# Spline layer: the part right of the middle added to x by VectorE in twelve units of sixteen

## The chip, the cores and the metric

The program runs on one core of one Trainium2 chip. The metric is the time of one execution of the whole program on the device, in microseconds, as the median of three runs. A core has a matrix engine (TensorE, "PE" in the profile; its weight loads are "PEld"), a vector engine (VectorE, "DVE"), an activation engine (ScalarE, "ACT"), GpSimd ("POOL") and SyncE ("SP"), which here issues DMAs. Each works through its own queue in order, and they wait for each other by semaphores.

## The reference

A network of four layers on x, 8 images of 64 channels of 128x128, all float32. Each layer is x = x + f(gn(x)) with a group norm in front. The layer that matters here is the second, a spline per channel:

```
x = x + _L0_conv_ref(_gn(x), ...)          # adder layer, 3x3, relu(b - sum|patch - w|)
x = x + _L1_conv_ref(_gn(x), ...)          # spline layer
x = x + _L2_conv_ref(_gn(x), ...)          # Haar, depthwise, 1x1, 3x3, gelu, inverse Haar
x = x + _L3_conv_ref(_gn(x), ...)          # nearest of 512 vectors

def _L1_conv_ref(x, coef, scale_base, scale_sp, bias):
    basis = _bspline_basis(xcl[..., None], grid)        # cubic, 8 functions on 12 knots
    spline = jnp.einsum('bhwck,ck->bhwc', basis, coef)
    out = scale_base * jax.nn.silu(xcl) + scale_sp * spline + bias
```

## The kernel before, in words

The eight images are worked on as four pairs: two images of 64 channels fill the 128 partitions. `run` takes a pair through layer 0, beside which the layers 2 and 3 of the pair before run as a list of steps, and then through layer 1 (`layer1`), which runs alone. After the last pair, layers 2 and 3 run by themselves. So layer 1 makes four separate stages in the profile. In layer 0 the order of the instructions on PE, ACT and DVE is written out by hand; in layer 1 it is left to the framework's scheduler, which orders each engine's queue by its own estimate, so that the instructions of `end` don't stand where the program has them.

Layer 1 cuts a pair's 128x128 pixels into 16 units of 8 rows (1024 pixels; 128x1024 per tile). The spline is even and odd about its middle: with z = |distance from the middle|, six truncated cubes of z serve the left and the right half. A tile holds one image, its 64 channels twice, so that the upper 64 partitions take knots 0 to 2 and the lower ones knots 3 to 5. For each unit and each of two images:

- z by ACT (L794) from xd, which DMA brings in (L747, four DMAs of 256 KB a unit, three buffers; beside them x itself, 1024 KB for two units);
- for three pairs of knots (p = 0, 1, 2) the truncated difference r, by ACT as a ReLU (L803) or by DVE as min and subtract (L805); its square by ACT into r3 (L806); and the cube r3 = r3 * r by DVE (L807). r has three buffers, r3 five;
- products by PE (L818): the cubes times coefficients into two PSUM tiles, `pa` (what holds left of the middle) and `pb` (what is added right of it), two buffers each. In float32 a product appears as two matmul records; those of the two images stand beside each other in halves of the array. With the second knot pair (p = 1) go the products of silu (L812, ACT) into `pa` (L820).

`end(n)` finishes a unit, and is called in the middle of the next one, after its second knot pair: DVE makes u = (x >= mean) * pb (L772), PE adds u to `pa` by a product with the identity (L774), and DVE writes x = pa + bias + x (L775). Two units make a chunk: after the second, DVE takes its statistics (L450, four instructions), and a chunk's x is stored by a DMA (L780). u has one buffer. In the last unit `end` stands by itself at the end of the stage.

Of the kernel before, what the change touches and what calls it, by code (L numbers as in the profile page):

```python
# [16 lines left out]
ALU = mybir.AluOpType  # L17
# [13 lines left out]
NQ = 6  # L31
# [69 lines left out]
class Net:  # L101
# [627 lines left out]
    def layer1(self, mr, stats, nxt):  # L729
        nc, tc = self.nc, self.tc  # L730
        N = R * W // 2
        images = [slice(i * C, (i + 1) * C) for i in range(2)]
        with ExitStack() as ctx:
            sp = ctx.enter_context(tc.tile_pool(name="l1", bufs=2))
            xdp = ctx.enter_context(tc.tile_pool(name="l1_xd", bufs=3))
            cp = ctx.enter_context(tc.tile_pool(name="l1_c", bufs=1))
            pp = ctx.enter_context(tc.tile_pool(name="l1_ps", bufs=2, space=PSUM))

            def unit(n):
                return self.x[n // 2][:, n % 2 * R // 2 : (n % 2 + 1) * R // 2, :].rearrange("p r w -> p (r w)")  # L740

            def twice(n):

                xd = xdp.tile([P, 2, N], F32, name="xd")
                for i in range(2):
                    for h in range(2):
                        nc.sync.dma_start(out=xd[images[h], i, :], in_=self.x_of[0][images[i], n * N : (n + 1) * N])  # L747
                if n % 2 == 0:
                    self.x.append(self.load(n // 2))
                return xd  # L750

            l1w = cp.tile([P, L1W], F32, name="l1w")
            nc.sync.dma_start(out=l1w, in_=self.l1w_dram)
            dspl = l1w[:, 0 : 10 * C].rearrange("p (k n c) -> p k n c", k=2, n=5)
            dbase, of_image = l1w[:, 10 * C : 12 * C], l1w[:, 12 * C :].rearrange("p (i n) -> p i n", i=2)
            self.x = []
            xds = [twice(n) for n in range(3)]

            sb = cp.tile([P, 2], F32, name="sb")
            nc.vector.tensor_copy(sb[:, 0:1], mr[:, 1:2])  # L760
            nc.vector.tensor_scalar(sb[:, 1:2], mr[:, 0:1], mr[:, 1:2], -1.0, ALU.mult, ALU.mult)
            zb = cp.tile([P, 2, 2], F32, name="zb")
            for i in range(2):
                pm = pp.tile([P, 2, 512], F32, name="pm", tag="pa")
                nc.tensor.matmul(pm[:, 0, 0:2], of_image[:, i, :], sb, start=True, stop=True)
                nc.vector.tensor_scalar(zb[:, i, :], pm[:, 0, 0:2], 2.5, None, ALU.mult)

            def end(n, pa, pb):

                xv = unit(n)  # L770
                u = sp.tile([P, N], F32, name="u", bufs=1)
                nc.vector.scalar_tensor_tensor(u, xv, mr[:, 0:1], pb.rearrange("p q n -> p (q n)"), ALU.is_ge, ALU.mult)  # L772
                for q in range(2):
                    nc.tensor.matmul(pa[:, q, :], self.ident, u[:, q * 512 : (q + 1) * 512], start=False, stop=True)  # L774
                nc.vector.scalar_tensor_tensor(xv, pa.rearrange("p q n -> p (q n)"), self.bias1, xv, ALU.add, ALU.add)  # L775
                if n % 2 == 1:
                    j = n // 2
                    self.chunk_stats(stats, j)
                    if nxt is not None:
                        nc.sync.dma_start(out=self.x_of[1][:, j * R * W : (j + 1) * R * W], in_=self.x[j].rearrange("p r w -> p (r w)"))  # L780

            late = None
            for n in range(2 * NCH):
                xv = unit(n)

                def work(name, bufs=2):
                    return sp.tile([P, N], F32, name=name, tag=name, bufs=bufs)

                pa = pp.tile([P, 2, 512], F32, name="pa")
                pb = pp.tile([P, 2, 512], F32, name="pb")  # L790
                zs = []
                for i in range(2):
                    z = work(f"z{i}")
                    nc.scalar.activation(z, xds[n][:, i, :], AF.Abs, bias=zb[:, i, 1:2], scale=zb[:, i, 0:1])  # L794
                    zs.append(z)
                for p in range(NQ // 2):
                    cubes, ws = [], []
                    for i in range(2):
                        r, r3 = work("r", 3), work("r3", 5)
                        kn = self.knots[:, p : p + 1]  # L800
                        on_act = p < 1 + i
                        if on_act:
                            nc.scalar.activation(r, zs[i], AF.Relu, bias=kn, scale=-1.0)  # L803
                        else:
                            nc.vector.tensor_scalar(r, zs[i], kn, kn, ALU.min, ALU.subtract)  # L805
                        nc.scalar.activation(r3, r, AF.Square)  # L806
                        nc.vector.tensor_tensor(r3, r3, r, ALU.mult)  # L807
                        cubes.append(r3)
                        ws.append(p + 3 if on_act else p)
                    if p == 0:  # L810
                        sl = work("sl")
                        nc.scalar.activation(sl, xv, AF.Silu, bias=sb[:, 1:2], scale=sb[:, 0:1])  # L812
                    for q in range(2):
                        cols = slice(q * 512, (q + 1) * 512)
                        for k, to in enumerate((pa, pb)):
                            for i in range(2):
                                stop = k == 1 and p == NQ // 2 - 1
                                nc.tensor.matmul(to[images[i], q, :], dspl[:, k, ws[i], :], cubes[i][:, cols], start=(p == 0), stop=stop)  # L818
                        if p == 1:
                            nc.tensor.matmul(pa[:, q, :], dbase, sl[:, cols], start=False, stop=False)  # L820
                    if p == 1 and late is not None:
                        end(*late)
                late = (n, pa, pb)
                if n == 4 and nxt is not None:
                    self.pad_first(nxt)
                if n + 3 < 2 * NCH:
                    xds.append(twice(n + 3))
            end(*late)


# [536 lines left out]
```

## Time and profile before

| | |
|---|---|
| time of three runs | 19147.62, 19152.85, 19155.82 us; median 19152.85 |
| profiled execution | span 19147.4 us from first to last instruction; no other time is shown for it |
| PE busy | 18332.0 us (96%) |
| DVE busy | 17951.2 us (94%) |
| ACT busy | 17340.8 us (91%) |
| POOL busy | 2778.2 us (15%) |
| L774 (identity product) | 256 matmul records, 592 ns median |
| L772, L775 (DVE, 128x1024 with PSUM) | 64 each, 1272 and 1284 ns median |
| L807 (DVE, 128x1024, two inputs in SBUF) | 384, 1218 ns median |
| wait of L775 for L774 | 91.3 us in 60 waits |

The page adds up an engine's busy time over the whole span, which here is an average over layer-0 stretches, four layer-1 stages and a tail. A matmul's duration includes its way through the array, and the next one starts before it ends; DVE and ACT instructions overlap a little, too. So what an instruction takes from its engine is read from the distance between starts, and a stage is looked at by itself. "issue" is idle time in which nothing visible was waited for.

### The profile page before, as it was taken

The numbers are of one execution on the slowest core, as the hardware profiler recorded it, in microseconds if no ns is written. First come the engines' busy times: TensorE is split into PE (matmuls) and PEld (weight loads), VectorE is DVE, ScalarE is ACT, GpSimd is POOL, SyncE is SP. The second block draws the span as 40 slices with busy tenths as digits, with TensorE's granted clock in tenths as the row PEclk, the third lists the DMA queues.
The fourth block names the chain that finished last, engine by engine and source line by source line (L and its number), as shares of the span: only waits on it lengthen the run. The fifth ranks groups of instructions, "written<-read, shape, count | busy, mean of one in ns | idle before, by whom it ended". The sixth has DMA issues, their size and how long they took to land.

```text
span 19147.4 us, 330733 instructions
## 1 busy us (share of the span) xinstructions
PE 18332.0 (96%) x146698; PEld 5818.3 (30%) x146698; DVE 17951.2 (94%) x13918; ACT 17340.8 (91%) x6457; POOL 2778.2 (15%) x1663
## 2 busy tenths in 40 slices
PE   8999999999999999999999999999999999999977
PEld 2333233232233222222222322222232323222263
DVE  8999999989999999998999999999899999999867
ACT  7999999889999999988999999998899999999803
POOL 0000000000000244300000034420000003442005
PEclk9999999999999999999999999999999999999986
DMA  2000000121111001021111100002011110000231
GB/s 66 6 11 10 6 10 8 40 68 32 40 34 33 25 18 29 25 61 48 34 42 30 33 21 24 23 28 78 29 35 41 35 34 16 22 25 13 62 96 39
DMA packets 425513, 636.07 MB, mean 33 GB/s; under 512 B 65168, under 2 KB 314640, under 8 KB 399120
## 3 DMA queue, kind: packets, MB, share of 16 engines
q1 hardware_dynamic: 368272, 549.81, 9.5%
q0 software_dynamic: 55808, 65.11, 1.9%
q8 instruction: 1149, 18.83, 0.4%
q14 instruction: 284, 2.33, 0.0%
HBM read 485.16 MB, written 129.54 MB: 32 GB/s over the span
## 4 chain that ended last, share of the span: by engine, by line
PE 53%; DVE 28%; issue 10%; ACT 8%; DMA 1%; SPq 0%; POOL 0%; DVEq 0%; ACTq 0%; POOLq 0%
PE ps L722 39%; DVE buf L655 12%; DVE buf L659 9%; ACT buf L653 7%; PE cv L1139 5%; PE pa L818 2%; PE pb L818 2%; DVE dw L1116 1%; DVE nd L1264 1%; DVE ix L1266 1%; DVE dw L897 1%; PE py L1162 1%; DVE x L655 1%; ACT t L1254 1%; PE pd L1252 1%
## 5 line engine op out<-in xcount | busy, mean ns | idle before, releaser
L722 PE MATMUL ps<-buf,sel 128*32 128x512 f32 x116336 | 13030.5, 597 | 371.1 <-DVE buf L659 234.2
L653 ACT ACTIVATE buf<-buf,w 128x4096 f32<-128x4096 f32 x1980 | 7213.9, 3710 | 301.8 <-PE ps L722 295.3
L653 ACT ACTIVATE buf<-x,w 128x4096 f32<-128x4096 f32 x1938 | 7046.2, 3710 | 347.0 <-PE ps L722 288.0
L722 PEld LDWEIGHTS ps<-buf,sel 128*32 128x32 f32 x116336 | 3625.9, 110 | 9365.5 <-issue 7898.4
L655 DVE TENSOR_SCALAR buf<-buf,w 128x4096 f32<-128x4096 f32 x1795 | 4162.2, 2356 | 188.7 <-PE ps L722 187.5
L655 DVE TENSOR_SCALAR buf<-x,w 128x4096 f32<-128x4096 f32 x1558 | 3639.5, 2366 | 287.4 <-PE ps L722 271.2
L659 DVE SCALAR_TENSOR_TENSOR buf<-buf,w,buf 128x2048 f32<-128x2048 f32 x1262 | 2913.4, 2348 | 22.9
L659 DVE SCALAR_TENSOR_TENSOR buf<-x,w,buf 128x2048 f32<-128x2048 f32 x1072 | 2475.3, 2349 | 19.7
L1267 POOL DMA_INDIRECT g<-in_L_conv_embed_weight,ix x768 | 1832.8, 2386 | 2840.3 <-issue 1400.3
L633 POOL DMA_DIRECT2D y<-in_x x480 | 608.8, 2099 | 9431.2 <-ACT y L620 6457.2
L1139 PE MATMUL cv<-dw,w2s 64*128 64x512 f32 x6912 | 1654.0, 606 | 3.2 <-issue 3.2
L653 ACT ACTIVATE x<-buf,w 128x4096 f32<-128x4096 f32 x396 | 1468.9, 3709 | 59.3 <-PE ps L722 59.3
L722 PE MATMUL ps<-x,sel 128*32 128x512 f32 x10832 | 1303.0, 594 | 27.1 <-DVE x L659 18.5
L1139 PEld LDWEIGHTS cv<-dw,w2s 64*128 64x128 f32 x6912 | 627.4, 186 | 1025.4 <-issue 1011.1
L655 DVE TENSOR_SCALAR x<-buf,w 128x4096 f32<-128x4096 f32 x281 | 659.9, 2348 | 24.6 <-PE ps L722 24.4
L722 PEld LDWEIGHTS ps<-x,sel 128*32 128x32 f32 x10832 | 350.8, 110 | 851.1 <-issue 747.5
L1116 DVE SCALAR_TENSOR_TENSOR dw<-sub,dws,dw 128x512 f32<-128x512 f32 (+2 forms) x768 | 574.5, 748 | 10.6
L1264 DVE CUSTOM_DVE_ANT_0 nd<-pd,t 128x512 f32<-128x512 f32 x768 | 519.8, 677 | 31.0 <-ACT t L1254 31.0
L807 DVE TENSOR_TENSOR r<-r,r 128x1024 f32<-128x1024 f32 x384 | 454.9, 1218 | 80.2 <-ACT r L806 72.2
L1266 DVE FIND_INDEX8 ix<-best,nd 128x8 uint32<-128x512 f32 x768 | 526.1, 685 | 0.1
L1252 PE MATMUL pd<-embT,xn 64*128 64x512 f32 x1536 | 490.1, 650 | 29.1 <-DVE best L1264 28.7
L1254 ACT ACTIVATE t<-esq_half,xsq 128x512 f32<-128x512 f32 x768 | 510.8, 717 | 3.1 <-DVE best L1264 3.1
(239 smaller groups left out, 7891.7 us busy)
## 6 DMA issues: line engine op xcount, KB each, us to landing
w2s<-w_dram SPq DMA_DIRECT2D x576, 192.0 KB
xd<-x_dram SPq DMA_DIRECT2D x256, 256.0 KB
x<-x_dram SPq DMA_DIRECT2D x56, 1024.0 KB
u<-u_dram SPq DMA_DIRECT2D x64, 768.0 KB
raw<-in_x SPq DMA_DIRECT2D x32, 1024.0 KB
x_dram<-y SPq DMA_DIRECT2D x512, 64.0 KB
out<-x SPq DMA_DIRECT2D x32, 1024.0 KB
y<-in_x POOLq DMA_DIRECT2D x480, 64.0 KB, 4.2
```

The costliest lines, as they stand in the source:

```text
L653: nc.scalar.activation(ab, tap(j, ts[0]), AF.Abs, bias=w[:, ts[0] : ts[0] + 1], scale=-1.0)
L655: nc.vector.tensor_scalar(ab, tap(j, ts[0]), w[:, ts[0] : ts[0] + 1], None, ALU.max)
L659: nc.vector.scalar_tensor_tensor(at, tap(j, t, h), w[:, t : t + 1], at, ALU.max, ALU.add)
L722: nc.tensor.matmul(at, sel[:, M - 1 - m : 3 * M - 1 - m], rhs, start=(n == first[p]), stop=(n + 1 == first[p + 1]))
L818: nc.tensor.matmul(to[images[i], q, :], dspl[:, k, ws[i], :], cubes[i][:, cols], start=(p == 0), stop=stop)
L1116: nc.vector.scalar_tensor_tensor(out, v, wt, out, ALU.mult, ALU.add)
L1139: nc.tensor.matmul(ps[:, i], weights[r, w // 3, :], v, start=(k == 0 and n == 0), stop=(k == 3 and n == 8))
L1252: nc.tensor.matmul(ps, xns[j][at, r, :], self.embT[at, :], start=True, stop=True)
L1254: nc.scalar.activation(t, self.esq_half, AF.Identity, bias=xsqs[j][:, n : n + 1])
L1264: nc.vector.tensor_tensor_reduce(nd, ps, t, 1.0, -FAR, ALU.subtract, ALU.max, mx[:, 0:1])
L1266: nc.vector.max_index(ix, mx, nd)
L1267: nc.gpsimd.indirect_dma_start(out=g[:, img, :], out_offset=None, in_=self.embed, in_offset=bass.IndirectOffsetOnAxis(ap=ix[:, 0:1], axis=0),)
```

## The change

In twelve of sixteen units (all but 3, 7, 11 and 15) DVE adds x to u in place, and L775 adds that sum instead of x; the product with the identity is left out. In those units the last product of the third knot pair into `pa` is marked as the one that ends the sum. Nothing else is edited.

```diff
+            def on_array(n):
+                return n % 4 == 3
+
             def end(n, pa, pb):
 
                 xv = unit(n)
                 u = sp.tile([P, N], F32, name="u", bufs=1)
                 nc.vector.scalar_tensor_tensor(u, xv, mr[:, 0:1], pb.rearrange("p q n -> p (q n)"), ALU.is_ge, ALU.mult)
-                for q in range(2):
-                    nc.tensor.matmul(pa[:, q, :], self.ident, u[:, q * 512 : (q + 1) * 512], start=False, stop=True)
-                nc.vector.scalar_tensor_tensor(xv, pa.rearrange("p q n -> p (q n)"), self.bias1, xv, ALU.add, ALU.add)
+                if on_array(n):
+                    for q in range(2):
+                        nc.tensor.matmul(pa[:, q, :], self.ident, u[:, q * 512 : (q + 1) * 512], start=False, stop=True)
+                    plus = xv
+                else:
+                    nc.vector.tensor_tensor(u, u, xv, ALU.add)
+                    plus = u
+                nc.vector.scalar_tensor_tensor(xv, pa.rearrange("p q n -> p (q n)"), self.bias1, plus, ALU.add, ALU.add)
...
-                                stop = k == 1 and p == NQ // 2 - 1
+                                stop = p == NQ // 2 - 1 and (k == 1 or not on_array(n))
```

## The prediction

> **What bounds the kernel now.** I first read the page's chain by line: the layer-1 matmuls of L818 have 4% of the 19147.4 us span, the adder layer's (L722) 39%. So the change can touch only the four stages of the spline layer. The table by stretches, asked for those four, says how large they are and who is busy:
>
> ```profile
> core 0: us, PE busy (x) PEld busy (x) DVE busy (x) ACT busy (x) POOL busy (x), PEclk, DMA share, GB/s
> 3801.00:4049.00 248.00, 240.40 (x896) 78.19 (x896) 203.34 (x206) 200.77 (x193) 0.00 (x0) 0.98 0.47 135
> 17922.00:18168.00 246.00, 236.81 (x896) 77.49 (x896) 203.48 (x207) 197.81 (x191) 0.91 (x5) 0.98 0.36 94
> ```
>
> About 990 us in all; TensorE (PE) is busy nearly throughout, VectorE (DVE) and ScalarE (ACT) some 82%. Busy matmuls are pipelined, so the chain of waits has to confirm it. Inside a stage it runs on PE alone; one unit of it:
>
> ```profile
> 3999.99 0.86 PE pb L818 x4
> 4000.85 0.86 PE pa L818 x4
> ...
> 4009.28 1.06 PE pa L820 x2
> 4010.34 1.72 PE pa L774 x4
> 4012.05 1.01 PE pa L818 x4
> ```
>
> The identity product (L774) is four matmul records, 1.72 us, on the path. DVE's timeline of the same unit shows what it does meanwhile and what it waits for (in brackets):
>
> ```profile
> 4001.96 1.27 DVE L772 SCALAR_TENSOR_TENSOR u<-x,mr,pb 128x1024 f32<-128x1024 f32 x1
> 4003.15 1.22 DVE L807 TENSOR_TENSOR r<-r,r 128x1024 f32<-128x1024 f32 x1
> 4004.29 1.53 DVE L805 TENSOR_SCALAR r<-z,knots 128x1024 f32<-128x1024 f32 x2
> 4006.54 3.50 DVE L807 TENSOR_TENSOR r<-r,r 128x1024 f32<-128x1024 f32 x3 [0.72 <-ACT r L806]
> 4009.95 0.81 DVE L805 TENSOR_SCALAR r<-z,knots 128x1024 f32<-128x1024 f32 x1
> 4012.09 1.28 DVE L775 SCALAR_TENSOR_TENSOR x<-pa,bias,x 128x1024 f32<-128x1024 f32 x1 [1.33 <-PE pa L774]
> 4013.29 2.35 DVE L807 TENSOR_TENSOR r<-r,r 128x1024 f32<-128x1024 f32 x2
> 4015.56 0.69 DVE L450 BATCH_NORM_STATS2 stats<-x 128x6 f32<-128x512 f32 x1
> 4016.16 1.27 DVE L772 SCALAR_TENSOR_TENSOR u<-x,mr,pb 128x1024 f32<-128x1024 f32 x1
> ```
>
> L775 starts at 3982.88, 3997.31, 4012.09, 4026.52: a unit takes 14.43 or 14.78 us, 14.61 in the mean. The extra 0.35 us is PE waiting once, near 4004.4, for a cube from L807.
>
> **The change, part by part.** Twelve units of sixteen lose L774; four (3, 7, 11, 15) keep it.
>
> *Removed from PE*: 4 records, 1.72 us a unit. PE's own work falls from 14.43 to 12.71 us.
>
> *Added to DVE*: one addition, 128x1024 f32, two inputs and output in SBUF: the shape of L807. Its mean duration is 1.218 us, but what it takes from the queue is the distance to the next start: three from 4006.54 to 4009.95, 3.41/3 = 1.135 us. Counted so, a unit's DVE work is six L807 (6 x 1.135 = 6.81), three L805 (4009.95 and its like, 0.72 each: 2.16), L772 (4001.96 to 4003.15: 1.19), L775 (4012.09 to 4013.29: 1.20) and two statistics on average (0.60 each: 1.20): 12.56 us. The cycle from 4001.96 to 4016.16 agrees: it has one statistics instruction, so 11.96, plus its two waits of 0.72 and 1.33 and 0.17 of overlap lost at them (1.218 - 1.135, twice) = 14.18 of 14.20 us. With the addition: 13.69 us. The trace shows no back-to-back chain L772, addition, L775; its nearest row is the stage's end, where statistics follow the L775 whose output they read: 4040.95 to 4042.27, 1.32 instead of 1.20 us. Two such steps cost at most 0.24 us a unit, and nothing if a cube is placed between them. I take nothing, since cubes stand next to L772 in the rows above, and keep 0.24 for the range.
>
> The Trainium skill, "VectorE: DVE Perf Modes", section "The DRAIN you can't avoid", says the next instruction doesn't start until the pipeline is empty. Taken so, every instruction costs its full duration: 13.65 us now and 14.87 with the addition, above 14.61, and the change would lose 0.26 us a unit. The rows speak against it: an L807 starts every 1.135 us although it lasts 1.218.
>
> *ACT*: unchanged; the same table for 3985.50 to 4014.75 (two units) has it busy 24.94 us, 12.47 a unit.
>
> *Moved*: nothing is issued elsewhere; no DMA is added. The last write to pa becomes the L818 of the third knot pair, so L775 waits for that alone and its 1.2 to 1.3 us wait for L774, with finished cubes queued behind it, goes. The scratch tile u was read by PE and is now read by DVE itself. Loads of xd and stores of x may go out some per cent faster; the stage uses 0.47 of the DMA engines at most, and inside the stage ACT waited for xd only at the start: nothing.
>
> *What is late next*: DVE, 13.69 us against PE's 12.71 and ACT's 12.47. Twelve units gain 14.61 - 13.69 = 0.92 each: 11.0 us a stage. In the three units that still hold an identity product beside the next unit's work, PE needs 14.43 us, L775 waits as now, and I charge the slower of today's two spacings: 3 x 0.17 = 0.5 us lost. The fourth (unit 15) stands at the stage's end, unchanged. So 10.5 us a stage, 42 us for four.
>
> The span of the profiled execution is 19147.4 us, the only time shown for it; the median is 19152.85, 5.5 us above. The difference is applied to the median: 19152.85 - 42 = **19111 us**.
>
> **Rivals.** *The gain is half lost to order (A).* The program's layer 1 has its order per engine fixed by the framework's scheduler, not by hand. If the addition lands between L772 and the cube L807 that PE waits for (4003.15 above), two things follow. The wait of 0.72 or 0.46 us at 4006.54 stays (that cube needs a square from ACT, behind a ReLU that needs the buffer freed at 4003.15): DVE's unit becomes 13.69 + 0.6 = 14.3. And the loop PE first matmul of pair 1, to the end of pair 2 (3989.86 to 4000.85 in the chain less 1.72: 9.27), square (1.1), L772, addition, cube (1.19 + 1.135 + 1.27) is 13.97: not the bound. Gain 0.3 x 12 - 0.5 = 3.1 a stage, 12 us: 19141. With both dependent steps back to back in a good order: (0.92 - 0.24) x 12 - 0.5 = 7.7, 31 us: 19122. For A speaks that L772 is placed before that cube now; against it, that a ready cube stands close by. Both ends lie within 0.2% (38 us, about what a measurement of this kernel can tell from no change).
>
> *The mix evens out (B).* If DVE works ahead during the units on PE, the mean counts: (12 x 13.69 + 4 x 12.56)/16 = 13.41, 1.2 us under 14.61, 15 units a stage, 72 us: 19081. Against it: five r3 buffers for six cubes a unit leave little room, and L775's wait stops DVE.
>
> *Slower, by the clock (C).* PE will now wait about once a unit, 12.71 against 13.7 to 14.3: 1.0 to 1.6 us. Elsewhere in this trace a short wait was followed by half clock:
>
> ```profile
> 7696.70:7700.10 3.40, 1.57 (x10) 0.29 (x2) 3.40 (x2) 3.40 (x2) 0.00 (x0) 1.00 0.00 0
> 7700.10:7706.90 6.80, 5.30 (x18) 1.29 (x22) 6.70 (x14) 5.95 (x4) 3.50 (x2) 0.50 0.02 5
> ```
>
> PE was busy 1.57 of 3.40 us, and the next stretch ran at 0.50. So a wait of 1.8 us was enough here. If order A holds and PE's wait falls whole into one such stretch and exceeds some 1.7 us, 3.4 us of matmuls take twice as long: 1.7 us more on the loop. 14.3 + 1.7 = 16.0, a loss of 1.4 us in twelve units: 67 us, 19220. Against it: with 13.7 us a unit the wait is 1.0, leaving 2.4 busy of 3.4.
>
> The Trainium skill, "TensorE: Matmul & The Clock Gate", section "HAM oscillation — how this bites in real kernels", gives the limit as an idle gap over about 3.4 us; by it C could not occur and its loss would be nothing. The rows just shown put the point lower, so C stays.
>
> *That the change doesn't do what it says* can hardly be: the choice by unit number holds in every pair.
>
> **How the numbers follow.** Forecast 0.46, 19095 to 19120; A 0.32; B 0.08; C 0.12; 0.02 for anything else. Faster by over 0.2% (below 19114.5) are B and most of the forecast: 0.48. Within 0.2%: A and the rest: 0.40. Slower: C, 0.12. The range runs from B, 19081, to 12 us above no change, 19165, for an order a little worse than A's; C is left out.
>
> **What would show it.** L774's records fall from 256 to 64 and a new DVE group of 48 additions appears at 1.22 us. In a stage, L775 should repeat every 13.7 us with PE idle about 1 us a unit, waiting for L807, its clock at 1.00; DVE over 95% busy; L775's 91.3 us of waits for L774 should fall to about a quarter. Wrong would be: a wait for ACT's squares left at 0.5 us or more a unit (A), half clock inside the stages (C), or spacings of 13.4 us (B).

## The result, and the profile after

The changed kernel takes 19247.71 us (median of five runs, 19244.63 to 19259.65), the kernel before 19154.63 us on the same chip (19147.62 to 19156.57). The ratio is 1.0049, 95% interval 1.0038 to 1.0060: **slower by 0.49%, 93 us**. The forecast was 42 us faster, with a range up to 19165; the sign is wrong. The profiled execution has a span of 19242.8 us, 95.4 us above that of before.

Lines have moved: the chain "u, identity product, write of x" was L772, L774, L775 and is L775, L778, L783; the addition is L781. Min L805 is now L813, square L806 is L814, cube L807 is L815, the products L818 and L820 are L826 and L828.

The first part of the page of after gives the busy time of each engine:

```profile
PE 18381.5 (96%) x146506; PEld 5842.3 (30%) x146506; DVE 18006.9 (94%) x13966; ACT 17341.3 (90%) x6457; POOL 2774.6 (14%) x1663
```

DVE has 55.7 us more, about 48 additions of 1.218 us (58.5). PE lost 192 records of the identity product, 82.6 us by 1.72 us for four, and yet its busy time rose by 49.5 us. Busy PE is not PE at its full rate, and that is the first sign that the order of its work changed. The same two stages as in the prediction, first and last, in the table by stretches of after (columns as there):

```profile
3802.00:4072.00 270.00, 251.59 (x848) 84.86 (x848) 216.56 (x218) 200.92 (x193) 0.00 (x0) 0.98 0.43 124
17995.00:18262.00 267.00, 247.42 (x848) 82.33 (x848) 218.23 (x220) 196.46 (x190) 0.91 (x5) 0.98 0.32 86
```

A stage has grown from about 247 to 269 us, with 48 matmul records fewer and the clock where it was, 0.98. Measured from the first z to the end of the last write of x, the four stages were 248.6, 247.7, 247.9 and 245.3 us and are 271.0, 269.1, 269.1 and 266.9: 989.5 against 1076.1. These 86.6 us are nearly all of the 95.4.

The unit is no longer even. DVE's timeline of after shows the spacing of the writes of x (L783), 20.09 us here, and what stands between two of them:

```profile
3968.41 0.80 DVE L813 TENSOR_SCALAR r<-z,knots 128x1024 f32<-128x1024 f32 x1
3971.09 1.28 DVE L775 SCALAR_TENSOR_TENSOR u<-x,mr,pb 128x1024 f32<-128x1024 f32 x1 [1.88 <-PE pb L826]
3972.29 2.35 DVE L815 TENSOR_TENSOR r<-r,r 128x1024 f32<-128x1024 f32 x2
3974.56 1.22 DVE L781 TENSOR_TENSOR u<-u,x 128x1024 f32<-128x1024 f32 x1
...
3976.83 1.28 DVE L783 SCALAR_TENSOR_TENSOR x<-pa,bias,u 128x1024 f32<-128x1024 f32 x1
3978.03 0.81 DVE L813 TENSOR_SCALAR r<-z,knots 128x1024 f32<-128x1024 f32 x1
...
3985.16 1.23 DVE L815 TENSOR_TENSOR r<-r,r 128x1024 f32<-128x1024 f32 x1 [3.20 <-ACT r L814]
...
3996.92 1.27 DVE L783 SCALAR_TENSOR_TENSOR x<-pa,bias,u 128x1024 f32<-128x1024 f32 x1
```

L775 is queued before `pb` is finished: DVE stands for 1.88 us with the cube that PE wants next right behind it. In before's rows L772 had no wait at all. The next min (L813) comes only after the addition and the write of x. ACT's timeline of after shows who waits for that min:

```profile
3978.93 1.06 ACT L814 ACTIVATE r<-r 128x1024 f32<-128x1024 f32 x1 [4.03 <-DVE r L813]
3979.89 1.23 ACT L802 ACTIVATE z<-xd,zb 128x1024 f32<-128x1024 f32 x1
3982.94 1.24 ACT L820 ACTIVATE sl<-x,sb 128x1024 f32<-128x1024 f32 x1 [1.83 <-PE pa L828]
3984.09 1.04 ACT L814 ACTIVATE r<-r 128x1024 f32<-128x1024 f32 x1
```

The square at 3978.93 waits 4.03 us for its min. The square of the other image stands behind a silu (L820) that waits 1.83 us more for PE, so DVE's cube at 3985.16 waits 3.20. The chain of waits in this window, which in before ran on PE alone, now changes engine (start, duration, what):

```profile
3970.20 0.87 PE pb L826 x4
3971.07 0.03 issue
3971.09 1.28 DVE u L775
3972.37 1.15 DVE r L815
3973.52 0.04 issue
3973.56 1.08 PE pa L826 x4
```

From the last product into `pb` to the next group of four, 2.49 us, the chain leaves PE: DVE's u, then the cube behind it. No product of this unit needs u. Some 10 us later it leaves PE again, in the rows shown above: the silu at 3982.94, the square at 3984.09, the cube at 3985.16 and PE at 3986.44. PE's timeline shows that it has only products of one image left meanwhile, two records at a time instead of four, and then stands idle, 1.04 us the first time and 1.68 the second.

DVE's lines in the first stage (3802 to 4072) show, behind the bar, how long DVE itself stands before them and for whom:

```profile
L815 DVE TENSOR_TENSOR r<-r,r 128x1024 f32<-128x1024 f32 x96 | 114.3, 1219 | 27.0 <-ACT r L814 27.0
L775 DVE SCALAR_TENSOR_TENSOR u<-x,mr,pb 128x1024 f32<-128x1024 f32 x16 | 20.5, 1279 | 25.1 <-PE pb L826 25.1
L783 DVE SCALAR_TENSOR_TENSOR x<-pa,bias,x 128x1024 f32<-128x1024 f32 x4 | 5.1, 1284 | 2.1 <-PE pa L778 2.1
```

These waits are 54.2 us. With the prediction's work for sixteen units, 12 x 13.69 + 4 x 12.56 = 214.5 us, they make 268.7 of the stage's 271.0. In before the same lines stand 45.1 us in the first stage (squares 19.1, L774 22.3, `pb` 3.7). So DVE got more work and its waits, which the prediction let shrink, grew.

Four waits, summed over the execution by the views of the lines concerned:

| who waits for what | before | after |
|---|---|---|
| u (L772, L775) for `pb` | 9.8 us in 8 | 101.8 us in 55 |
| ACT's square for DVE's min | 20.2 us in 32 | 165.9 us in 83 |
| PE's products for DVE's cube | 76.3 us in 51 | 228.8 us in 177 |
| write of x for the identity product | 91.3 us in 60 | 8.6 us in 6 |

The last row is the wait that the change was to remove; it went, to a tenth. Three others took its place. PE's time in the four stages can be laid out from the starts of its records, each taken as 0.43 us (0.86 for the four of a pair), with two that run beside each other counted once:

| PE in the stages, us | before | after |
|---|---|---|
| products of cubes | 679.7 | 785.9 |
| identity product | 109.8 | 27.5 |
| products of silu | 109.8 | 109.8 |
| nothing started | 90.2 | 152.9 |
| sum | 989.5 | 1076.1 |

If every product had its partner of the other image beside it, the products of cubes would take 3072/2 x 0.43 = 660 us. Before was close to that. After, half of the array was often empty, which costs 106.2 us; PE's idle time grew by 62.7; 82.3 went: the sum is +86.6.

### The profile page after: what moved, and what is told of

Read it like the earlier page. It is cut to its first block, busy times and chain, and to the rows that moved or that the text cites. A ratio compares the mean times of both kernels' runs of the same rounds, so it can differ in the third digit from the quotient of the medians.

```text
span 19242.8 us, 330417 instructions
## 1 busy us (share of the span) xinstructions
PE 18381.5 (96%) x146506; PEld 5842.3 (30%) x146506; DVE 18006.9 (94%) x13966; ACT 17341.3 (90%) x6457; POOL 2774.6 (14%) x1663
## 4 chain that ended last, share of the span: by engine, by line
PE 52%; DVE 29%; issue 10%; ACT 8%; DMA 1%; SPq 0%; POOL 0%; DVEq 0%; ACTq 0%; POOLq 0%
PE ps L722 38%; DVE buf L655 12%; DVE buf L659 9%; ACT buf L653 6%; PE cv L1147 5%; PE pa L826 2%; PE pb L826 2%; DVE dw L1124 1%; DVE ix L1274 1%; DVE nd L1272 1%; DVE x L655 1%; PE py L1170 1%; DVE dw L905 1%; PE pd L1260 1%; PE pa L828 1%
## 5 line engine op out<-in xcount | busy, mean ns | idle before, releaser
L722 PE MATMUL ps<-x,sel 128*32 128x512 f32 x10832 | 1303.4, 594 | 27.5 <-DVE x L659 18.9
L655 DVE TENSOR_SCALAR x<-buf,w 128x4096 f32<-128x4096 f32 x281 | 659.9, 2348 | 24.9 <-PE ps L722 24.7
L826 PE MATMUL pa<-r,l1w 128*64 128x512 f32 x1536 | 534.9, 612 | 70.9 <-DVE r L815 70.8
L814 ACT ACTIVATE r<-r 128x1024 f32<-128x1024 f32 x384 | 389.9, 1046 | 203.2 <-DVE r L813 165.9
L815 DVE TENSOR_TENSOR r<-r,r 128x1024 f32<-128x1024 f32 x384 | 457.2, 1219 | 102.5 <-ACT r L814 102.4
```

Source lines behind the costliest of these rows:

```text
L655: nc.vector.tensor_scalar(ab, tap(j, ts[0]), w[:, ts[0] : ts[0] + 1], None, ALU.max)
L722: nc.tensor.matmul(at, sel[:, M - 1 - m : 3 * M - 1 - m], rhs, start=(n == first[p]), stop=(n + 1 == first[p + 1]))
```

## The experiments

Two things differ between the kernels: the work, and the order of the queues that the scheduler makes of it. I asked first whether the order of PE's queue is the cause (the products of the two images queued one after the other instead of in pairs) or the added work of DVE, and later whether it is any one queue at all. Each group of kernels shares its runs of before, on one chip; a difference is always to the before of the same chip.

### Either half alone, and PE's queue fixed

e1 takes the changed kernel and lets PE's queue in layer 1 keep the order of the text; e2 does the same to the kernel before.

```diff
+            ctx.enter_context(tc.manual_schedule(engines={ET.PE}))
```

> The change, with PE's queue in layer 1 kept in the order in which the program is written; VectorE's and ScalarE's order is still the scheduler's. In the built program all 384 groups of four products then have the two images side by side; with the change as it is 225 of 384 have, in the kernel before 373. Theory 1 (the changed order on PE split the pairs, so that half the array works at a time): the spline products cover some 660 us instead of 786, and the time falls by at least that difference less new waits, to 19110 to 19150 us. Theory 2 (the added 48 instructions make VectorE too slow, whatever the order): it stays within 20 us of 19248. Theory 3 (VectorE stands before L775 while finished cubes wait behind it): some of the loss stays, 19160 to 19200.

> The kernel before, with PE's queue in layer 1 in written order (all 384 groups paired instead of 373): the control for e1. Theory 1: 11 groups at some 0.7 us, at most 8 us faster, 19145 to 19155 us. Theories 2 and 3 say nothing of it beyond no change. If it were as much faster as e1 is against the change, the written order would be a gain by itself and e1 would prove nothing about the change.

e1: 19207.35 us against 19155.17, ratio 1.0028 (1.0018 to 1.0038). e2: 19151.98, 0.9998 (0.9988 to 1.0008). In the stages e1 returned 44 of the 87 us: 1031.8. Its products of cubes fell from 785.9 to 706.2 us, but PE's idle time rose from 152.9 to 188.4. So with PE's queue paired half of the delay stays, and much of it shows as waiting instead. The median lies 7 us above the range of theory 3. The test isn't clean: with PE's queue written, the scheduler also put the instructions of DVE and ACT in another order than in the change, so the 44 us can't be given to the pairs alone. e2 is before again, as expected.

e3 leaves the identity product out of the twelve units and adds nothing to DVE (the part right of the middle is missing there); e4 keeps every identity product and adds a sum that nobody reads.

```diff
 e3, from the changed kernel
-                    nc.vector.tensor_tensor(u, u, xv, ALU.add)
-                    plus = u
+                    plus = xv
 e4, from the kernel before
+                if n % 4 != 3:
+                    w = sp.tile([P, N], F32, name="w", bufs=1)
+                    nc.vector.tensor_tensor(w, u, xv, ALU.add)
```

> One part alone: the identity product is dropped in twelve units and nothing is put in its place, so the part right of the middle is left out there. Order by the scheduler. Work is only removed, 82 us of PE and none added. In the built program 124 groups are split against 11 before. Theory 1: 113 split groups at some 0.7 us take back about 80 us: 19120 to 19180. Theory 2: without the addition VectorE has 12.56 us a unit and PE 12.71, so 1.5 us in twelve units: 19070 to 19090.

> The other part alone: all sixteen units keep the identity product, and in twelve VectorE makes the sum u + x as well, into a tile that nobody reads. Order by the scheduler; 97 groups are split against 11 before. Theory 1: 86 more split groups at some 0.7 us: 19200 to 19230. Theory 2 in the form of the prediction's sums (VectorE 13.69 us under PE's 14.43): no change, 19145 to 19165; in the form that the addition is too much for VectorE: as slow as the change, 19240 or more.

e3: 19185.92, ratio 1.0016 (1.0007 to 1.0026). It does strictly less work than before and is 31 us slower; the writes of x come, in one stretch, 15.5, 24.9, 7.8 and 12.8 us apart. e4: 19233.31, ratio 1.0041 (1.0026 to 1.0055), 78 us slower, though DVE's 13.69 us a unit should have fitted under PE's 14.43. Neither theory's range holds e3's number (that of theory 1 ends 6 us below), and e4 lies 3 us above theory 1's range and far from a sum in which DVE's work fits. That a removal costs time can hardly come from the work; it points at the order, which the next kernels test.

### The same work in an order held by hand

For these the body of layer 1 is written as small functions, called in an order that I chose, and all three queues keep it. The loop, with `cut` for ReLU or min, `choose` for u, `on_pe` for the identity product, `plus` for the addition, `finish` for the write of x:

```
for n in range(NU):
    cube(n, 1, 1); products(n, 1); on_pe(n - 1)
    cut(n, 2, 0); cut(n, 2, 1); cut(n + 1, 0, 0)
    square(n, 2, 0); square(n, 2, 1)
    plus(n - 1)
    cube(n, 2, 0); cube(n, 2, 1); products(n, 2)
    square(n + 1, 0, 0); cube(n + 1, 0, 0)
    finish(n - 1)
    cut(n + 1, 0, 1); zed(n + 2, 0); square(n + 1, 0, 1)
    cut(n + 1, 1, 0); cube(n + 1, 0, 1); products(n + 1, 0)
    square(n + 1, 1, 0); cut(n + 1, 1, 1); zed(n + 2, 1)
    some_stats(2)
    cube(n + 1, 1, 0); square(n + 1, 1, 1); silu(n + 1)
    choose(n)
    ...                                        # loads of xd for unit n + 3
```

e5 is the change in this order (`on_array(n)` is `n % 4 == 3`), e6 the work of before (`True`), e7 the addition in all sixteen units (`False`), e8 the change with the addition moved:

```diff
+                plus(n - 1)
                 cube(n, 1, 1)
...
-                plus(n - 1)
                 cube(n, 2, 0)
```

> The change, with layer 1's order on PE, VectorE and ScalarE written out by hand: all groups paired, L772 of a unit just before the last cube of the next unit's second knot pair, the addition in the gap before the cubes of the third pair, L775 after the next unit's first cube, two statistics a unit. This is the order that the prediction's sum took for granted (that of the kernel before, with the addition in its gap). Theory O (the whole loss is in the order that the scheduler made; the work itself is worth what the sum says): 13.7 us a unit, 14.4 to 14.8 beside an identity product, PE waiting about 1 us a unit: 19095 to 19125 us. Theory 2 (the addition is too much work for VectorE): 14.6 us a unit or more, 19155 and above.

> The same order by hand, with the identity product in all sixteen units: the control for e5. PE needs 14.43 us a unit: Theory O expects 14.4 to 14.6 us a unit, as in the kernel before, 19140 to 19160 us. If it comes out as fast as e5, the order and not the change is the gain.

> The same order by hand, with the addition on VectorE in all sixteen units. Theory O with the prediction's sum: 13.69 us in every unit and no unit that waits for L774, so a little faster than e5, by up to 3 x 0.9 + some 1 us at the stage's end, 15 us over four stages: 19085 to 19115. If the mix evens out (VectorE works ahead in the units on PE), e5 is the faster of the two by up to 15 us.

> As e5, with one instruction moved on VectorE: the addition stands right behind L772, ahead of the cube that PE waits for (the prediction's rival A). By the sum there: 14.0 to 14.3 us instead of 13.7 in twelve units, 0.3 to 0.6 us each: 14 to 29 us slower than e5. If the place of one instruction cost nothing, the two would agree within 5 us, and order would matter only through PE's pairs.

On a chip whose before takes 19175.49: e5 19151.12, ratio 0.9988 (0.9979 to 0.9997); e6 19236.07, 1.0032 (1.0020 to 1.0043); e7 19128.11, 0.9975 (0.9965 to 0.9984); e8 19196.52, 1.0010 (1.0001 to 1.0019).

e5 and e7 repeat every 13.69 us wherever the unit has an addition: the prediction's sum for DVE, to the last digit. Both times lie above the expected ranges; less the 20 us by which before is slower on this chip, e7 lies inside its range and e5 6 us above. e6 misses: 15.50 us a unit where 14.4 to 14.6 was expected. DVE's timeline of e6 (L843 is the write of x, L833 the identity product) shows why:

```profile
8617.57 1.28 DVE L843 SCALAR_TENSOR_TENSOR x<-pa,bias,x 128x1024 f32<-128x1024 f32 x1 [2.06 <-PE pa L833]
```

My order put the write of x too early for units with an identity product. DVE's 12.56 us, this wait of 2.06, one of 0.72 for a square as in the prediction's rows, and the two lost overlaps of 0.085 make 15.51. So e6 is no fair partner of e5, and the three in e5 that hold an identity product take 15.49 for the same reason.

e8 is the prediction's rival A by itself: the addition between u and the cube that PE waits for. It repeats every 14.62 us. DVE's timeline of e8 (L828 is u, L837 the addition, L803 the cube, L799 the square):

```profile
8623.45 1.27 DVE L828 SCALAR_TENSOR_TENSOR u<-x,mr,pb 128x1024 f32<-128x1024 f32 x1
8624.76 1.22 DVE L837 TENSOR_TENSOR u<-u,x 128x1024 f32<-128x1024 f32 x1
8625.90 1.22 DVE L803 TENSOR_TENSOR r<-r,r 128x1024 f32<-128x1024 f32 x1
...
8629.28 1.23 DVE L803 TENSOR_TENSOR r<-r,r 128x1024 f32<-128x1024 f32 x1 [0.72 <-ACT r L799]
```

The addition reads what the instruction before it writes, and starts 1.31 us after it instead of 1.19. With 13.69, 0.12 for that, 0.72 for the wait and 0.085 for the overlap, the unit is 14.62. One misplaced instruction costs 0.93 us a unit, all of the gain; against e5 the median is 45 us higher, where 14 to 29 were expected. This is still not the loss of the change.

e9 and e10 mend the order: `finish(n - 1)` of a unit with an identity product stands just ahead of `products(n + 1, 0)`. e9 is the change, e10 the work of before. e11 is e7 with the products queued image by image; e12 is the change with the addition in all sixteen units, ordered by the scheduler.

```diff
 e9, e10
-                finish(n - 1)
+                if not on_array(n - 1):
+                    finish(n - 1)
...
                 cube(n + 1, 0, 1)
+                if on_array(n - 1):
+                    finish(n - 1)
 e11
-                    for k, to in enumerate((pas[n], pbs[n])):
-                        for i in range(2):
+                    for i in range(2):
+                        for k, to in enumerate((pas[n], pbs[n])):
 e12, from the changed kernel
-                return n % 4 == 3
+                return False
```

> As e5, but in the units with an identity product L775 stands one min and one cube later on VectorE, just before PE needs the tile pa again. In e5 the unit beside an identity product took 15.49 us, with VectorE standing 2.1 us before L775 while a cube was ready. Theory H (that wait at the head of the queue is the whole of the excess): the unit comes down to PE's own 14.4 us and e9 is 3 x 1 us a stage, 10 to 14 us faster than e5. If the excess is PE's own work, nothing changes, within 5 us.

> The same move with the identity product in all sixteen units (e6 with L775 later). e6 took 15.50 us a unit against 14.61 of the kernel before by the scheduler. Theory H: 14.4 us a unit, PE without a pause, 60 to 66 us faster than e6 and within 0.1% of the kernel before or up to 10 us faster than it. Otherwise it stays at e6's time.

> As e7, with PE's products of every group of four issued image by image (left and right sums of image 0, then of image 1) instead of side by side: all 384 groups split, the same instructions otherwise. It measures the price of a split by itself. Theory 1: a group of eight records that took 1.72 us takes 0.7 to 1.7 us more; six groups a unit make PE 17 to 23 us instead of 12.7, so 3 to 9 us over VectorE's 13.69 in each of 64 units: 200 to 600 us slower than e7. If the two halves of the array run beside each other whatever the order in the queue, e11 is as fast as e7.

> The change carried to all sixteen units, with the order by the scheduler as in the change. 183 groups are split, against 159 with the change and 11 before. If the mix of two kinds of units is what upsets the scheduler's order, this is faster than the change; if it is the freed time on PE itself, it splits and waits as the change does or more: 19230 to 19290 us.

With before at 19154.91: e9 19122.66, ratio 0.9983 (0.9974 to 0.9992); e10 19156.21, 1.0002 (0.9993 to 1.0011); e11 19109.91, 0.9977 (0.9968 to 0.9986); e12 19253.65, 1.0053 (1.0037 to 1.0068).

e10 is before again: 14.43 us in every unit, stages of 988.9 us. So the rewritten text by itself neither gains nor loses. From e10 to e9 the work changes, and with it the place of one instruction in the twelve units, the write of x, which stands two DVE instructions earlier; all else keeps its order. The stages lose 42.9 us (988.9 to 946.0); the prediction said 42. The medians differ by 33.6. In e9 the unit beside an identity product was expected at 14.4 us; it takes 16.1, and the next one 11.8. DVE's timeline of e9 (L794 is the min) for a unit with an addition, 13.69 us from write to write:

```profile
8653.50 1.28 DVE L843 SCALAR_TENSOR_TENSOR x<-pa,bias,u 128x1024 f32<-128x1024 f32 x1
...
8658.87 1.27 DVE L828 SCALAR_TENSOR_TENSOR u<-x,mr,pb 128x1024 f32<-128x1024 f32 x1
8660.07 1.22 DVE L803 TENSOR_TENSOR r<-r,r 128x1024 f32<-128x1024 f32 x1
8661.20 1.53 DVE L794 TENSOR_SCALAR r<-z,knots 128x1024 f32<-128x1024 f32 x2
8662.65 1.22 DVE L837 TENSOR_TENSOR u<-u,x 128x1024 f32<-128x1024 f32 x1
8663.78 3.49 DVE L803 TENSOR_TENSOR r<-r,r 128x1024 f32<-128x1024 f32 x3
8667.19 1.28 DVE L843 SCALAR_TENSOR_TENSOR x<-pa,bias,u 128x1024 f32<-128x1024 f32 x1
```

No bracket: nothing waits. u comes when `pb` is done, the two mins of the third pair go ahead of the addition, and the addition ahead of the cubes covers the time that ACT needs for their squares.

e11 brings down the theory that split groups in PE's queue cost time by themselves. All 384 groups of four products are split, image after image, and it is as quick as e7: 13.69 us a unit, stages of 936.4 against 936.2. PE's timeline of e11, in rows of up to four products of one target:

```profile
8658.38 1.08 PE L822 MATMUL pa<-r,l1w 128*64 128x512 f32 x4
8659.24 1.08 PE L822 MATMUL pb<-r,l1w 128*64 128x512 f32 x4
```

Four records still take 0.86 us: when both cubes are there, the products of the second image run beside those of the first however the queue has them. So a half-empty array, as in after, is what a late cube looks like; the order of the two images in the queue is not enough to make one. That holds where both cubes are ready; with late cubes e11 doesn't test it. e12 shows that the mix of two kinds of units is not the cause either: without any identity product the scheduler's order has stages of 1089.3 us, against 936.2 for the same work in e7. In the same way the change's own work takes 1076.1 us in the scheduler's order and 946.0 in e9's.

### Which queue

Here the text of e9 is kept and fewer queues are held: e13 VectorE's alone, e14 those of TensorE and ScalarE, e15 none.

```diff
-            ctx.enter_context(tc.manual_schedule(engines={ET.PE, ET.DVE, ET.Activation}))
+            ctx.enter_context(tc.manual_schedule(engines={ET.DVE}))                      (e13)
+            ctx.enter_context(tc.manual_schedule(engines={ET.PE, ET.Activation}))        (e14)
                                                                              (e15: line left out)
```

> The program text of e9, but only VectorE's queue in layer 1 keeps its order; PE's and ScalarE's are the scheduler's. If VectorE's order carries the loss: within 20 us of e9, 19110 to 19145. If PE's or ScalarE's order does: 19180 and above.

> The program text of e9 with PE's and ScalarE's queues in written order and VectorE's by the scheduler. If VectorE's order carries the loss: at least 40 us slower than e9, 19165 to 19230. If not: within 20 us of e9.

> The program text of e9 with all of layer 1 left to the scheduler. If the scheduler orders by its own estimate whatever the text: as slow as the change, 19200 to 19270. If the order of the text is what it follows: within 20 us of e9, and the loss of the change would lie in where the text puts the end of a unit.

With before at 19154.78: e13 19114.57, ratio 0.9978 (0.9968 to 0.9988); e14 19111.53, 0.9978 (0.9968 to 0.9987); e15 19130.52, 0.9988 (0.9979 to 0.9998). Whichever queue is left free, the time stays low; even with all three free the scheduler makes a good order out of this text. So it is not that the scheduler can't order this work; it is what it makes of the text of the change. Since the loss is absent from e15 already, e13 and e14 can't say whether one queue alone carries it in the change, and of the kernels with the change's text only e1 fixes a single queue.

### Where the text calls the end of a unit

e16 keeps the text of the change literally on all three engines (the line of e1, with all three named). e17 and e18 edit one digit of the changed kernel and leave the order to the scheduler: the end of the unit before is called after the first, or the third, knot pair.

```diff
-                    if p == 1 and late is not None:
+                    if p == 0 and late is not None:      (e17)
+                    if p == 2 and late is not None:      (e18)
                         end(*late)
```

> The change with the order of its own text kept on PE, VectorE and ScalarE in layer 1: the end of a unit (L772, addition, L775 and all four statistics at once) stands after the second knot pair's cubes and before the third pair's mins. If that order is bad by itself: as slow as the change or worse, 19230 and above. If only what the scheduler makes of it is bad: 19110 to 19200.

> The change with one edit: a unit's end is called after the next unit's first knot pair instead of its second; order by the scheduler. If the place in the text decides, it moves the time by 30 us or more against the change, either way; if the scheduler's own estimate decides, it stays within 20 us of 19248.

> The same with the end called after the next unit's third knot pair. If the place in the text decides, the end of a unit then yields to the third pair's mins and cubes, and VectorE waits less before L775: 30 us or more faster than the change, 19120 to 19215. If the scheduler's estimate decides: within 20 us of 19248.

With before at 19178.28: e16 19754.69, ratio 1.0302 (1.0284 to 1.0319); e17 19307.80, 1.0068 (1.0051 to 1.0085); e18 19166.22, 0.9995 (0.9985 to 1.0004). The place of one call moves the time by 141 us with the same operations, and one knot pair later undoes the loss of the change.

Side by side, with two of the waits above:

| kernel | to its before, us | stages, us | u waits for `pb`, us | products wait for cubes, us |
|---|---|---|---|---|
| before | | 989.5 | 9.8 | 76.3 |
| the change | +93 | 1076.1 | 101.8 | 228.8 |
| e17, end after first pair | +130 | 1111.4 | 155.8 | 295.3 |
| e18, end after third pair | -12 | 970.3 | 29.9 | 126.1 |
| e12, all sixteen | +99 | 1089.3 | 129.6 | 358.0 |
| e4, only added | +78 | 1062.0 | 63.9 | 109.3 |
| e1, PE as written | +52 | 1031.8 | 61.7 | 277.2 |
| e3, only removed | +31 | 1010.4 | 105.8 | 217.4 |
| e15, other text | -24 | 948.2 | 22.0 | 121.2 |
| e9, by hand | -32 | 946.0 | 9.4 | 136.9 |
| e14, PE and ACT by hand | -43 | 936.0 | 7.5 | 142.5 |

The wait of u for `pb` parts the rows: over 60 us in all six kernels that lose time, 30 us at most in the others. It rises with the earlier call and falls with the later one. It isn't alone in this: ACT's squares wait for mins 81.4 to 252.5 us in the same six and 27.2 to 69.5 us in e18, e15, e9 and e14. Nor does it measure the loss: e3 waits 105.8 us for `pb` and loses 31 us, the change 101.8 and 93. Products also wait for cubes in the quick ones, where DVE has more work a unit than PE.

e16 is slow by itself: with the text kept literally no engine works ahead, ACT waits 677.5 us for mins, and the wait of u is only 19.4. So the text's order is not what the scheduler makes of it; the scheduler's own order is far better than that, and merely worse than before's.

## Why the prediction was wrong

**The step that failed** is "*What is late next*: DVE, 13.69 us", and with it "Twelve units gain 14.61 - 13.69 = 0.92 each". It takes DVE's work for the length of a unit, so it puts DVE's waits in those units at nothing. They could be nothing only if every other instruction kept its place ("nothing is issued elsewhere"), although the text had said that layer 1's order is the scheduler's. The runs showed a mean of 16.30 us between writes instead of 13.69, and 54.2 us of waits of DVE in the first stage, more than the 45.1 of before: 25.1 for `pb` and 27.0 for squares. The small term beside it held: it took nothing for the addition because cubes would stand next to L772, and in all 48 units of the change a cube stands right ahead of the addition, never u.

**What was right.** The work. DVE's unit of 13.69 us was measured as 13.69 in e5, e7, e9 and e11; with the order held but for one write, the stages gain 42.9 us (e10 to e9) where 42 was predicted. That the totals agree so closely is partly luck: e10's unit is 14.43 us, not 14.61, and e9's four units average 13.83, not 13.96, so sixteen units gain 9.6 us a stage instead of 10.5; the ends of the stage bring it to 10.7. L774's records fell to 64, the additions take 1.212 to 1.221 us, and the write's wait for L774 fell (8.6 us, less than the quarter that was predicted). Counting by the distance between starts was right too: in e11's stretch 8600 to 8740 DVE is busy for 140.00 of 140.00 us, and a unit takes 13.69 us, not the 14.87 that full durations would give. The Trainium skill's section "The DRAIN you can't avoid" in "VectorE: DVE Perf Modes" adds that a next instruction that is not held starts earlier. The rows agree with that half: 1.135 us after a start when the data are independent, 1.31 after u when the addition reads it.

**Terms that were mis-sized.** The three units with an identity product beside others' work were charged 14.78 us; in e9's order one such unit and the next take 16.1 and 11.8, a mean of 13.97, in e5's 15.49. Hence e9's mean of 13.83.

**Rival A** named the right danger in the wrong size. It moved one instruction, and gave 14.3 us a unit and 19141. e8 measures that case as 14.62: the wait is 0.72 rather than the mean of 0.6, and the dependence and the lost overlap add 0.2. The real change moved u, the mins and the squares as well: 14.06 to 20.09 us between writes. **Rival C** gave 19220, the number nearest to 19247.71, for a reason that didn't occur: the clock of the stages is 0.98 as before, and from 3830 to 4060, in the first stage, PE's products wait 1.7 us at most (its weight loads 2.6) at a clock of 1.00. That it came nearest is luck. Its price also took one row for more than it shows. PE was idle for 1.83 us of the stretch to 7700.10, but that wait went on behind the stretch's end. PE's timeline of before:

```profile
7697.15 1.12 PE L1252 MATMUL pd<-embT,xn 64*128 64x512 f32 x2
7701.60 2.07 PE L1252 MATMUL pd<-embT,xn 64*128 64x512 f32 x2 [3.33 <-DVE best L1264]
```

The wait was 3.33 us, and half clock began 1.83 us into it; no wait that ended after 1.8 us is shown there.

**Rival B** did not appear in any order: the repeating units of every kernel average 13.69 us or more.

**What is shown and what isn't.** Shown: the loss is in the four stages; it is not the work (e9 and e15 do the same work 130 and 128 us quicker in the stages, e7 that of e12 153 us), not the clock, not a split queue of PE by itself (e11), not the mix of units (e12). It is the order that the scheduler gives to the text of the change, and the place of the call of `end` moves it (e17, e18). Argued from the waits, not shown: that u queued too early on DVE and mins queued behind the end of a unit are what delays it. Both go with the loss in the scheduler-ordered kernels of the table, neither has its size, and no kernel moved u or the mins by themselves within the scheduler's order. Open: whether one queue of the change carries the loss, how much of e1's 44 us is PE's pairs, and why the scheduler chose this order. A few us between stages and whole times stay open, too: e9 and e11 differ by 9.6 us in the stages and by 12.8 in the medians, but not in the spans of their profiled executions (19115.7 and 19115.6).

**A version that beats both**: e11 and e14 take 45 and 43 us less than their before (0.9977 and 0.9978, intervals below 0.9987). The addition is worth having with a good order, held by hand or made by the scheduler from the rewritten text (e15, 24 us less than its before); with only the call moved (e18, 0.9985 to 1.0004) the gain isn't clear of the noise.

## What to carry to other kernels

Where a scheduler orders the queues, an edit is two changes, one of work and one of order, and the trace of before prices only the first. Before trusting the sum, ask what becomes ready at the place where the text calls it and what would then stand behind it in each queue; the cheapest test is the same edit with one call moved, or with the order held on both sides. In these kernels the quick orders (e9, e14, e15) have two mins, which feed ACT, between u and the addition, where the change has one or none; and e8 shows what one instruction ahead of a cube costs. Here an instruction that nobody waits for did best behind those that feed another engine.

## What the runs showed of the hardware

- Products into the two halves of the array ran beside each other even when queued image by image (0.86 us for four records in e11, as in pairs).
- In e16 the clock inside the stages fell: 0.88 in the stretch 8700 to 8840, where one wait of PE's products for a cube lasted 6.9 us. In the changed kernel, with waits of up to 1.7 us from 3830 to 4060, the clock stayed at 1.00.
- The Trainium skill, "TensorE: Matmul & The Clock Gate", section "HAM oscillation — how this bites in real kernels", puts the limit at gaps over about 3.4 us. That fits the changed kernel, but not all of e16: from 8703.00 to 8706.40 the clock was 0.50, and the longest wait of PE in the ten us before was 2.06 us, ending at 8701.70. After another wait of 2.06 us, ending at 8844.96, the clock was 1.00 (8842.90 to 8846.30). The prediction's wait of 3.33 us lies just under the page's limit, with half clock 1.83 us into it. What decides isn't shown.
- The kernel before takes about 19155 us on the chips of three groups of experiments (e1 to e4, e9 to e12, e13 to e15) and 19175 to 19178 us on those of the two others, a difference as large as several of the effects above; only differences on one chip were compared.
